# The router's product with the router as the stationary operand: four token groups on four column groups, and one transpose back

## The chip, the cores and the metric

The kernel runs on one core of a Trainium2 chip. Its engines are TensorE (PE in the profile, with its weight loads listed apart as PEld), VectorE (DVE), ScalarE (ACT), GpSimd (POOL), and SyncE (SP), which here only issues DMAs. The metric is the device time of one execution in microseconds (us).

## The reference

The input x has 4 sequences of 1024 tokens with 256 channels. Four blocks follow one another, each on a layer norm of x and each added to x: a retention, a mixture of experts, an RWKV-6 block, and the same mixture of experts again. The change lies in the first two lines of the mixture of experts:

```python
logits = t @ Wg.T + bg                      # t: 4096 x 256, Wg: 8 x 256
probs = jax.nn.softmax(logits, axis=-1)
topw, topi = jax.lax.top_k(probs, K)        # K = 2 of 8 experts
topw = topw / jnp.sum(topw, axis=-1, keepdims=True)
def body(acc, packed):                      # once for each expert
    w1e, w2e, ce = packed
    gate, up = jnp.split(t @ w1e.T, 2, axis=-1)
    return (acc + ce[:, None] * ((silu(gate) * up) @ w2e.T), None)
```

All numbers are float32. The logits are 4096 x 8, once for each of the two mixtures.

## The kernel before

Tokens go in 8 blocks of 512, each of four groups of 128 (NT = 4); channels go in two halves of 128 (KC = 2). The router's logits are made once for each block and each of the two mixtures, so there are 16 calls, and they lie scattered over the stages:

- In the retention stage (up to about 345 us) six calls for the first mixture, put in after chosen chunks of the loop over 32 chunks (lines 1518 and 1531).
- In the first mixture (345 to 570 us) two calls, between expert tiles (line 1558, tiles 7 and 9). This stage goes through 71 tiles of 128 tokens: turn the tile (`fetch`), multiply by w1 (`up`), turn the activation, multiply by w2 (`down`), and scatter.
- In the RWKV stage (about 660 to 1270 us) six calls for the second mixture. That stage is a loop of 64 steps (8 blocks of 8) of scans on VectorE and products on GpSimd, with TensorE's work laid between them by hand (tables `amid`, `late`, `uses`, and lines 1626 to 1629 for the router).
- In the second mixture (from about 1270 us) two calls (lines 1663 and 1558).

One call has four parts. `tokens` normalizes the four groups on ScalarE (line 533). `turned` (line 544) turns them by eight TensorE transposes, and two ScalarE copies bring the result to SBUF as `m_tT`, channels on the partitions (lines 237 and 238). `product` (line 554) multiplies, and `biased` (line 562) adds the bias on VectorE and writes `m_logit`. Outside the RWKV stage `logits` (line 549) runs the first three in a row, and `biased` follows at once. In the RWKV stage they are spread over the steps: `product` is issued at the end of step 8n+19, `biased` in the middle of step 8n+20.

In `product` the turned tokens are the stationary operand (128 x 128) and the router, 128 x 8, is streamed: 8 matmuls, each with its own weight load. A float32 matmul leaves two rows in the trace, so a call has 16 rows of LDWEIGHTS and 16 of MATMUL.

The order on TensorE and ScalarE is the order of the program text everywhere (line 1471). VectorE and GpSimd are ordered by a scheduler in the retention stage and by the text after it (line 1541); SP's queue is ordered by the text in the RWKV stage. [...]

The PSUM tiles named "mm" are a ring of three banks: a new one waits until the one three before it has been read. The router's weight `wr` is loaded by one DMA near the start (line 1457); behind it on SP's queue are the bias and the weights of the retention.

Two other places of the kernel use the form of matmul that the change brings in, a 128 x 32 stationary operand with the result on 32 partitions: the retention's `a_yp` (line 370) and the RWKV stage's `w_varp` (line 1214).

Of the kernel before, what the change touches and what calls it, by code (L numbers as in the profile page):

```python
# [39 lines left out]
F32 = mybir.dt.float32  # L40
# [5 lines left out]
P = 128  # L46
B, T, C = 4, 1024, 256
KC = C // P
BLK = 512
NB = T // BLK  # L50
NT = BLK // P
H, D = 16, 16
GH = P // D
E = 8
# [54 lines left out]
def hybrid_kernel(  # L109
# [24 lines left out]
    nc = tc.nc  # L134
    mm = nc.tensor.matmul
# [3 lines left out]
    def pool(name, side="left"):  # L139
        return tc.alloc_tile_pool(name=name, bufs=1, side=side, reuse_waits="tile")  # L140
# [4 lines left out]
    keep = pool("keep")  # L145
# [3 lines left out]
    def psum(shape, name, tag="mm"):  # L149

        t = ps.tile([P, 512], F32, name=name, tag=tag, bufs=3 if tag == "mm" else 1)
        n = int(np.prod(shape[1:]))
        if len(shape) == 2:
            return t[:, :n]
        return t[:, :n].rearrange("p (a b) -> p a b", b=shape[2])
# [18 lines left out]
    ident = cst[:, O_ID : O_ID + P]  # L174
# [14 lines left out]
    def weight(src, name, where):  # L189
        n = src.shape[1]  # L190
        t = where.tile([P, KC, n], F32, name=name)
        nc.sync.dma_start(out=t, in_=src.rearrange("(k p) n -> p k n", p=P))
        return t
# [296 lines left out]
    class Piece:  # L490
# [58 lines left out]
        def logits(self, n):  # L549
            self.tokens(n)  # L550
            self.turned()
            self.product()

        def product(self):
            tT = self.tT
            lp = self.lp = psum([P, NT, E], "m_lp")
            for i in range(NT):
                for c in range(KC):
                    mm(lp[:, i, :], lhsT=tT[:, c, i * P : (i + 1) * P], rhs=wr[:, c, :],  # L559
                       start=(c == 0), stop=(c == KC - 1))  # L560

        def biased(self, n):
            nc.vector.tensor_add(
                self.logit[:, n * NT : (n + 1) * NT, :], self.lp,
                bias.unsqueeze(1).to_broadcast([P, NT, E]),
            )

# [376 lines left out]
    def rwkv(pi, w):  # L944
# [65 lines left out]
        def deltas(j, parts):  # L1010
# [15 lines left out]
            def mixed(late=False):  # L1026
                for f, c, dp in dps:
# [12 lines left out]
                    if f > 0:  # L1040
                        nc.gpsimd.tensor_add(xf, xf, d["now"][:, c, :])  # L1041

            return [lambda f=f, c=c: product(f, c) for f, c in parts], mixed

        def decay(j):
# [408 lines left out]
            )  # L1454


    wr = weight(router, "wr", keep)
    bias = keep.tile([P, E], F32, name="bias")
    nc.sync.dma_start(out=bias, in_=router_b.partition_broadcast(P))
    ph = pool("ph")  # L1460
# [46 lines left out]
    m, mid = moes[0].pieces[:2]  # L1507
# [42 lines left out]
    def add(j, f, *a):  # L1550
        extra.setdefault(j, []).append((f, *a))

    def pieces_sent(mid, end, logits):

        for i in range(mid.nt):
            add(4 + i, mid.send, i)
        for n, j in logits:
            add(j, end.logits, n)
            add(j, end.biased, n)
        for n in range(PARTS):  # L1560
            add((9, 9, 10, 11, 11, 11)[n], end.route)
        for i in range(end.nt):
            add(12 + i, end.send, i)
        add(6, mid.table, 0)
        add(7, mid.table, 1)
        add(14, mid.table, 2)
        add(18, end.table, 3)
# [44 lines left out]
    extra, mids, fronts = {}, {}, {}  # L1612
# [5 lines left out]
    for n in range(2 * HB - 1):  # L1618
        m = [p for p in moe.pieces if p.start <= n][-1]
        if n == 2 * HB - 2:  # L1620
            add(8 * n + 15, m.block, n - m.start)
            continue
        add(8 * n + 15, m.sums, n - m.start, 0)
        add(8 * n + 16, m.sums, n - m.start, 1)
        fronts[8 * n + 17] = [(m.sums, n - m.start, 2)]
        add(8 * n + 17, m.tokens, n - m.start, True)
        fronts[8 * n + 18] = [(m.turned,)]
        add(8 * n + 19, m.product)
        mids[8 * n + 20] = [(m.biased, n - m.start)]
    mids[44].append((next_a.route,))  # L1630
    add(44, next_a.route)
# [163 lines left out]
```

## Time and profile before

| | us |
|---|---|
| median of 3 runs | 1574.15 |
| lowest and highest of them | 1569.29, 1587.33 |
| the profiled execution, its own time | 1564.52 |
| its span, from the first to the last instruction | 1562.7 |
| busy: PE, DVE, POOL, ACT | 1346.6, 997.7, 892.1, 643.0 |
| mean granted TensorE clock | 0.911 |

Busy time by stage, from the table of windows: in the first 345 us PE is busy for 311.4 and DVE for 205.5; from 345 to 570 us PE for 199.9 and DVE for 101.4; from 660 to 1270 us PE for 501.7, DVE for 540.6 and POOL for 521.6; from 1270 to 1420 us PE for 132.9 and DVE for 61.1. So TensorE leads in the retention and in the mixtures, and VectorE and GpSimd lead in the RWKV stage.

The granted clock is that of TensorE, as a share of full speed. Idle time of an engine that is not the one that holds up the rest costs nothing, so a busy share alone does not tell what an instruction costs.

### The profile page before, as it was taken

Reading aid. Unit: us, or ns where it says so; the run is one execution under the profiler, and the core shown is the slowest. Engines: PE = TensorE matmul, PEld = TensorE weight load, DVE = VectorE, ACT = ScalarE, POOL = GpSimd, SP = SyncE. Lnnn points to the kernel's source line nnn. Section 1 sums busy time; section 2 is a strip of 40 time slices with the busy share of each in tenths; the row PEclk is TensorE's granted clock in tenths of the full one; section 3 lists DMA queues with packets and bytes.
Section 4 is the critical chain, followed back from the end, with each engine's and each line's share of the span. In section 5 each row is a group of like instructions: output and inputs, shape, how many; then the busy total and the mean of one; then the engine's idle time right before and its main releaser. Section 6 shows DMA issues by size and latency. Waiting matters only on the chain.

```text
span 1562.7 us, 21181 instructions
## 1 busy us (share of the span) xinstructions
PE 1346.6 (86%) x6684; PEld 710.2 (45%) x6684; DVE 997.7 (64%) x1914; ACT 643.0 (41%) x1630; POOL 892.1 (57%) x853
## 2 busy tenths in 40 slices
PE   5999999877999989998979798888796677999993
PEld 3667676554656644422233332333332234556561
DVE  6667556535443443299978787979998964433544
ACT  2343434443443333444545454544454224443331
POOL 4233321663573325399988888877799834653231
PEclk9999898978799999998979798979898679899997
DMA  8992111232333431267665454533555932332635
GB/s 291 326 323 84 48 48 42 69 119 69 122 128 100 132 116 54 63 148 190 169 138 148 114 144 109 146 97 108 131 159 135 263 99 67 116 115 85 193 126 185
DMA packets 117549, 207.72 MB, mean 133 GB/s; under 512 B 12192, under 2 KB 80000, under 8 KB 117440
## 3 DMA queue, kind: packets, MB, share of 16 engines
q1 hardware_dynamic: 95904, 160.20, 36.2%
q0 software_dynamic: 17184, 39.86, 8.2%
q10 hardware_dynamic: 4352, 6.29, 1.3%
q8 instruction: 57, 0.93, 0.3%
q14 instruction: 52, 0.43, 0.1%
HBM read 139.18 MB, written 67.14 MB: 132 GB/s over the span
## 4 chain that ended last, share of the span: by engine, by line
PE 56%; DVE 14%; POOL 13%; ACT 7%; issue 5%; DMA 3%; SPq 0%; POOLq 0%; DVEq 0%; ACTq 0%
PE m_hp L836 15%; PE m_op L873 7%; POOL w_s L1168 5%; DVE w_s L1160 5%; PE w_pp L1072 4%; PE a_qkp L311 3%; DVE w_vb L1158 2%; PE a_yp L370 2%; PE w_dp L1020 2%; PE m_xtp L829 2%; PE a_sp L350 2%; PE m_lp L559 2%; PE a_gp L293 2%; POOL xg_all L785 2%; PE m_atp L866 2%
## 5 line engine op out<-in xcount | busy, mean ns | idle before, releaser
L1168 POOL TENSOR_TENSOR w_s<-w_s,w_rT 128x1024 f32<-128x1024 f32 x128 | 304.3, 2412 | 43.2 <-DVE w_s L1160 31.5
L879 POOL DMA_INDIRECT y_all<-m_y,m_to x142 | 137.6, 969 | 284.3 <-ACT m_xt L831 164.9
L836 PE MATMUL m_hp<-w1a,m_xt 128*128 x568 | 285.8, 628 | 11.8 <-ACT m_xt L831 11.0
L842 DVE TENSOR_TENSOR m_a<-m_hp,m_sg 128x256 f32<-128x256 f32 x142 | 60.1, 424 | 266.7 <-ACT m_sg L840 266.7
L1160 DVE TENSOR_TENSOR_SCAN w_s<-w_wk,w_carry,w_vb 128x512 f32<-128x512 f32 x128 | 160.9, 1276 | 18.3 <-ACT w_carry L1178 8.4
L1158 DVE TENSOR_TENSOR w_vb<-w_vb,w_wk 128x1024 f32<-128x1024 f32 x128 | 153.1, 1196 | 17.0 <-ACT w_wk L1101 15.9
L1160 DVE TENSOR_TENSOR_SCAN w_s<-w_wk,w_vb 128x512 f32<-128x512 f32 x128 | 152.9, 1216 | 14.3 <-PE w_yp L1191 7.0
L873 PE MATMUL m_op<-w2a,m_aT 128*128 x568 | 149.2, 386 | 3.9 <-DVE m_aT L868 1.9
L785 POOL DMA_INDIRECT xg_all<-m_row,m_at x128 | 125.4, 980 | 43.7 <-issue 30.4
L836 PEld LDWEIGHTS m_hp<-w1a,m_xt 128*128 128x128 f32 x568 | 103.0, 202 | 87.6 <-issue 74.6
L1191 PE MATMUL w_yp<-w_s,core_c 128*32 128x512 f32 x512 | 93.9, 654 | 41.9 <-POOL w_s L1168 32.7
L840 ACT ACTIVATE m_sg<-m_hp 128x256 f32<-128x256 f32 x142 | 54.5, 384 | 163.6 <-PE m_hp L836 163.6
L323 POOL TENSOR_TENSOR a_t<-a_t,a_t 128x512 f32<-128x512 f32 x32 | 41.1, 1283 | 126.6 <-DVE a_t L322 103.7
L878 ACT ACTIVATE m_y<-m_op,m_share 128x256 f32<-128x256 f32 x142 | 67.3, 474 | 107.1 <-PE m_op L873 106.3
L873 PEld LDWEIGHTS m_op<-w2a,m_aT 128*128 128x128 f32 x568 | 98.2, 193 | 14.1 <-ACT m_y L878 3.0
L1038 POOL TENSOR_TENSOR w_xf<-w_xf,w_sx 128x512 f32<-128x512 f32 x60 | 77.9, 1298 | 35.8 <-ACT w_xf L1037 34.7
L353 DVE TENSOR_TENSOR a_pt<-a_sp,ret_c 128x2048 f32<-128x2048 f32 x32 | 73.2, 2286 | 17.3 <-PE a_sp L350 17.3
L866 PEld LDWEIGHTS m_atp<-cst,m_a 128*128 128x128 f32 x284 | 40.6, 145 | 84.0 <-issue 66.7
L1041 POOL TENSOR_TENSOR w_xf<-w_xf,w_xT 128x512 f32<-128x512 f32 x64 | 69.7, 1090 | 6.1 <-DVE w_xf L1035 1.4
L829 PE MATMUL m_xtp<-cst,m_xg 128*128 128x128 f32 x284 | 57.8, 287 | 13.2 <-DMA m_xg<-xg_all 13.2
L831 ACT COPY m_xt<-m_xtp 128x256 f32<-128x256 f32 x142 | 51.9, 366 | 37.1 <-PE m_xtp L829 37.0
L311 PE MATMUL a_qkp<-wqkv,a_xT 128*128 128x512 f32 x128 | 67.2, 652 | 0.0
(308 smaller groups left out, 2492.6 us busy)
## 6 DMA issues: line engine op xcount, KB each, us to landing
w_vb<-v_all SPq DMA_DIRECT2D x125, 512.0 KB
xg_all<-zero SPq DMA_DIRECT2D x34, 520.0 KB
m_xg<-xg_all SPq DMA_DIRECT2D x34, 520.0 KB
tab<-in_rope SPq DMA_DIRECT2D x32, 512.0 KB
m_back<-y_all SPq DMA_DIRECT2D x48, 256.0 KB
v_all<-w_vT SPq DMA_DIRECT2D x64, 128.0 KB
res<-in_x SPq DMA_DIRECT2D x8, 512.0 KB
w1a<-in_w SPq DMA_DIRECT2D x8, 512.0 KB
```

What stands on the lines that cost most here:

```text
L311: mm(qkp, lhsT=xc[:, c, cols], rhs=wqkv[:, c, 0 : 2 * C], start=(c == 0), stop=(c == KC - 1))
L353: nc.vector.tensor_mul(pts[i].rearrange("p j n t -> p (j n) t"), sp.rearrange("p j n t -> p (j n) t"), causal.unsqueeze(1).to_broadcast([P ...
L785: nc.gpsimd.indirect_dma_start(out=self.moe.sends[2 * (self.start * NT + i) + n][:, :], out_offset=bass.IndirectOffsetOnAxis(ap=self.at[n] ...
L829: nc.tensor.transpose(tp[:, c, :], self.xg[g][:, i, c * P : (c + 1) * P], ident)
L836: mm(hp, lhsT=self.xt[j][:, c, :], rhs=w1a[:, bass.ds(self.ev[j], 1), c, :].rearrange("p o n -> p (o n)"), start=(c == 0), stop=(c == KC - 1))
L873: mm(op, lhsT=self.aT[j][:, c, :], rhs=w2a[:, bass.ds(self.ev[j], 1), c, :].rearrange("p o n -> p (o n)"), start=(c == 0), stop=(c == KC - 1))
L879: nc.gpsimd.indirect_dma_start(out=self.scatters[j][:, :], out_offset=bass.IndirectOffsetOnAxis(ap=self.to[g][:, i : i + 1], axis=0), in_= ...
L1038: nc.gpsimd.tensor_mul(xf, xf, sx)
L1158: nc.vector.tensor_mul(vb, vb, wk[:, 1:2, :].to_broadcast([P, 2, BLK]))
L1160: nc.vector.tensor_tensor_scan(s[:, q, 1 : BLK + 1], wk[:, 0, :], vb[:, q, :], 0.0 if j % NB == 0 else st[j - 1]["carry"][:, n, 2 * h + q ...
L1168: nc.gpsimd.tensor_mul(s[:, :, 0:BLK], s[:, :, 0:BLK], d["r"][:, g, :].unsqueeze(1).to_broadcast([P, 2, BLK]),)
L1191: mm(d["yp", g][32 * q : 32 * q + 32, :], lhsT=w["sel"][:, i, :], rhs=d["s", n, q // 2][:, q % 2, 0:BLK], start=False, stop=(i == 3), skip ...
```

## The change

The router becomes the stationary operand, padded with zeros from 8 to 32 columns. Each of the four groups of 128 tokens streams through one of four column groups of the array, and its logits land, turned, on its own 32 of the 128 partitions of one PSUM tile. A new ScalarE copy brings that tile to SBUF (`m_lT`), and a new TensorE transpose, `flipped`, turns it back so that tokens lie on the partitions again; `biased` reads 8 of each 32 columns. The matmuls are still 8 per call, now with the channel half as the outer loop. A second "mm" tile is taken per call. In the RWKV stage `flipped` is put in the front of step 8n+20, between `product` and `biased`. The load of `wr` now waits for a memset on GpSimd.

```diff
@@ -550,18 +550,27 @@
             self.tokens(n)
             self.turned()
             self.product()
+            self.flipped()
 
         def product(self):
+
             tT = self.tT
-            lp = self.lp = psum([P, NT, E], "m_lp")
-            for i in range(NT):
-                for c in range(KC):
-                    mm(lp[:, i, :], lhsT=tT[:, c, i * P : (i + 1) * P], rhs=wr[:, c, :],
-                       start=(c == 0), stop=(c == KC - 1))
+            lp = psum([P, P], "m_lp")
+            for c in range(KC):
+                for i in range(NT):
+                    mm(lp[32 * i : 32 * i + 32, :], lhsT=wr[:, c, :],
+                       rhs=tT[:, c, i * P : (i + 1) * P], start=(c == 0), stop=(c == KC - 1),
+                       skip_group_check=True)
+            self.lT = ph.tile([P, P], F32, name="m_lT", tag="m_lT", bufs=1)
+            nc.scalar.copy(self.lT, lp)
+
+        def flipped(self):
+            self.lp = psum([P, NT, 32], "m_lpT")
+            nc.tensor.transpose(self.lp.rearrange("p i e -> p (i e)"), self.lT, ident)
 
         def biased(self, n):
             nc.vector.tensor_add(
-                self.logit[:, n * NT : (n + 1) * NT, :], self.lp,
+                self.logit[:, n * NT : (n + 1) * NT, :], self.lp[:, :, 0:E],
                 bias.unsqueeze(1).to_broadcast([P, NT, E]),
             )
 
@@ -1454,7 +1463,9 @@
-    wr = weight(router, "wr", keep)
+    wr = keep.tile([P, KC, 32], F32, name="wr")
+    nc.gpsimd.memset(wr, 0.0)
+    nc.sync.dma_start(out=wr[:, :, 0:E], in_=router.rearrange("(k p) n -> p k n", p=P))
@@ -1626,6 +1637,7 @@
         add(8 * n + 19, m.product)
+        fronts.setdefault(8 * n + 20, []).append((m.flipped,))
         mids[8 * n + 20] = [(m.biased, n - m.start)]
```

## The prediction

> **What bounds the kernel now.** I read the page first, the chain that ended last:
>
> ```profile
> PE 56%; DVE 14%; POOL 13%; ACT 7%; issue 5%; DMA 3%; SPq 0%; POOLq 0%; DVEq 0%; ACTq 0%
> PE m_hp L836 15%; PE m_op L873 7%; POOL w_s L1168 5%; DVE w_s L1160 5%; PE w_pp L1072 4%; PE a_qkp L311 3%; DVE w_vb L1158 2%; PE a_yp L370 2%; PE w_dp L1020 2%; PE m_xtp L829 2%; PE a_sp L350 2%; PE m_lp L559 2%; PE a_gp L293 2%; POOL xg_all L785 2%; PE m_atp L866 2%
> ```
>
> The product to be changed, m_lp at line 559, carries 2% of the chain, some 30 us. That is the ceiling. The view of its tile gives its size:
>
> ```profile
> L559 PEld LDWEIGHTS m_lp<-wr,m_tT x256: 186/192/338, 155.3 to 1331.1; 128*128 128x128 f32 x128
> L559 PE MATMUL m_lp<-wr,m_tT x256: 256/256/383, 155.3 to 1331.2; 128*128 128x8 f32 x128
> ```
>
> These are min/median/max ns. 256 rows over 16 calls are 16 rows per call; each streams only 8 columns, but loads a full 128x128 weight. Now one call after another, in the chain in order of time (start, length), the first call and then the seventh:
>
> ```profile
> 155.35 1.95 PE m_lp L559 x16
> 157.30 1.20 PE a_sp L350 x16
> ```
>
> ```profile
> 398.01 1.98 ACT m_xn L533 x4
> 400.04 0.44 PE m_xtp L237 x2
> 400.48 0.03 issue
> 400.51 3.58 PE m_lp L559 x16
> 404.10 0.52 PE m_xtp L829 x2
> ```
>
> The same 16 rows take 1.95 us in one and 3.58 in the other. The windows around the seventh call tell why (after the busy times, the column before the last two is the granted clock):
>
> ```profile
> 396.90:400.30 3.40, 1.60 (x9) 0.81 (x8) 2.16 (x9) 3.33 (x8) 2.59 (x3) 1.00 1.06 345
> 400.30:403.80 3.50, 3.47 (x18) 3.29 (x17) 0.00 (x0) 0.75 (x2) 2.91 (x6) 0.53 1.05 354
> 403.80:407.20 3.40, 3.40 (x8) 1.85 (x8) 1.83 (x6) 0.37 (x1) 2.05 (x2) 0.50 0.15 55
> 407.20:410.60 3.40, 3.40 (x14) 1.88 (x13) 0.76 (x2) 1.70 (x5) 0.96 (x1) 0.98 0.09 33
> ```
>
> The clock is 1.00 while PE waits for ScalarE and does thin transposes, then half for about 6.8 us, the product included. In one-microsecond windows I find such half-clock stretches at or after all ten calls outside the RWKV stage, in lengths near 3.4, 6.8 and 10.2 us. A call is therefore dear where the clock is halved, and cheap where it isn't.
>
> **What a new product costs.** The nearest row has exactly the new shape: w_varp, eight matmuls of a 128x32 weight with 128 columns, four column groups. The timeline shows one call of it at full clock and one at half:
>
> ```profile
> 828.17 0.66 PE L1214 MATMUL w_varp<-w_sq,tail_c 128*32 128x128 f32 x16
> 1211.11 1.10 PE L1214 MATMUL w_varp<-w_sq,tail_c 128*32 128x128 f32 x16
> ```
>
> A single row lasts 0.27 at full and 0.42 at half clock (273 median, 419 max), so rows follow at (0.66-0.27)/15 = 0.026 us and (1.10-0.42)/15 = 0.045 us. Sixteen rows fall from 1.95 to 0.66, and from 3.58 to 1.10. Were that all, the saving would be 1.3 to 2.5 us a call.
>
> **What takes it back.** First, the loop order. Before, the first two groups used both channel halves, eight rows, before PE needed the second half of m_tT. Now it is needed after four rows. The two copies stand in the timeline around the seventh call:
>
> ```profile
> 399.90 1.21 ACT L238 COPY m_tT<-m_xtp 128x512 f32<-128x512 f32 x2
> ```
>
> The second ends at 401.11, 0.60 after the product started; with the 0.04 that PE needs to follow, the other 12 rows start at 0.64. They end at 0.64 + 11x0.026 + 0.27 = 1.20 (full clock) or 0.64 + 11x0.045 + 0.42 = 1.56 (half). Second, the way back. ScalarE follows PE after 0.09 (the a_tp matmuls end at 159.54, their copy starts at 159.63). A 128x128 copy out of PSUM takes 0.273:
>
> ```profile
> L328 ACT COPY a_vz<-a_vp 128x128 f32<-128x128 f32 x64 | 14.0, 273 | 42.8 <-PE a_vp L315 42.8
> ```
>
> Then 0.04 back to PE, and one transpose, after which the next row can start in 0.11 (0.22 at half clock; m_xtp at 829 is chained at 0.22 for two rows, 0.52 in the slow stretch). PE is free at 1.71 us (full) or 2.18 (half), instead of 1.88 (157.23-155.35) or 3.44 (403.95-400.51). A copy could cost more: the Ln of the same tile takes 0.367, which would take 0.1 a call.
>
> The Trainium skill, "TensorEngine Tiling (Array Packing)", section PSUM Bottleneck, speaks against the change: after a fourfold gain on TensorE the copy out of PSUM may become the bottleneck. The rows agree in kind: of 1.71 us PE works for about 0.75. With TensorE's gain alone I would sum 1.3 x 4 full-clock-like and 2.5 x 6 slow calls, some 20 us; with the wait, less than half. I take the latter. The same page (Key Properties) says that a change of tiling mode drains TensorE. In the trace w_varp starts at 828.17, 0.43 after the start of the 512-column row ahead of it (0.59 long), so entering costs nothing visible; leaving leaves 0.20 without a weight load. By the rule, an estimate from one row's tail (0.27, twice per call) would be 16x0.54 = 9 us, all of the gain; here both switches fall into waits already counted, so I take 0, and keep 0.2 a call (3 us) for the range.
>
> **The sum, call by call** (gain in the time to the next PE work).
> - Retention, calls 1 to 5: 0.2; then 0.5, 0.7, 0.7, where the clock fell in mid-product (2.27, 2.53, 2.62 us before; about 1.7 to 1.8 now, as the work ends before or near the fall); 1.3 for the call at 322 us. Call 6 (345.3 us) is followed by a wait of PE for m_xg until 355.25: 0. Together 3.4.
> - First mixture, at 400 and 415 us: 1.25 each, 2.5.
> - RWKV, at 836, 914, 991, 1067 and 1149 us: off the chain, 0 (below). The sixth, at 1222 us, is on it (3.51 us, then w_rp, for which DVE waited 1.49): its m_tT is there beforehand and ScalarE idles, so 1.10+0.09+0.27+0.04+0.22 = 1.7 in place of 3.4, of which at most 1.5 counts.
> - Second mixture: 0.1 (1278 us, full clock) and 1.0 (1328 us, half for most).
> Sum 8.5 us.
>
> **The RWKV calls, and who stands behind the new waits.** At 836 us:
>
> ```profile
> 836.50 1.95 PE L559 MATMUL m_lp<-wr,m_tT 128*128 128x8 f32 x16
> 838.30 1.10 PE L1238 MATMUL w_rp<-w_rstd,tail_c 128*128 128x512 f32 x2
> 841.37 0.66 DVE L1245 TENSOR_TENSOR w_cen<-w_cen,w_rp 128x512 f32<-128x512 f32 x1
> ```
>
> The new copy stands on ScalarE behind the sums of w_xn and the w_carry copies (until 838.87), so `flipped`, and behind it on PE w_rp and w_twp, start about 1.0 us later. w_rp would end at 840.4 for a reader at 841.37: covered. w_twp ends at 844.0 rather than 843.0, w_tw and w_cen on ScalarE follow 1 us later, and GpSimd's w_sq (845.93 here, 923.53 at the second call, where w_cen ended at 922.63) may be late by some tenths. Bounds 0 and 1.0 a call; I take 0.3 x 5 = 1.5 us lost. If the cover is gone, 5. ScalarE's next work there (w_tw) waits for PE anyway, so the copy's wait holds nothing else up.
>
> **Edits I cost at nothing.** The memset of wr is one of POOL's first (those of the page's start end at 2.5 us), and SP reaches wr's load at 2.74; behind it on SP stand bias, ret_c, wqkv, wgate and the rest, of which wqkv is first needed at 14.84. If the memset came 2 us late, the slack takes it. The DMA moves the same elements. The additional "mm" tile doesn't lengthen any hold: m_lp is freed by the copy, and biased frees m_lpT three allocations before its bank is wanted, as before. 16 copies add 4.4 us to ScalarE, which is idle in those places. biased reads 32 elements as before (0.19 us). In the retention the scheduler could place biased differently on DVE; the next DVE work there, a_pt, waits for later PE work in any case. I leave ±2 us for that.
>
> Net: 8.5 - 1.5 = 7.0 us off. Against the profiled execution's own time, 1564.5 (span 1562.7 and 1.8 around it), that is 1557.5. The median of the runs shown lies 9.6 above that execution; I carry the difference over: 1574.15 - 7 = 1567.
>
> **The rivals.**
> *The half clock goes, too.* The m_lp rows fill about a half to a whole of the slow stretches, with 8 columns a row. If a dense burst ends a stretch one 3.4 us window sooner at six to nine calls, that is 1.7 us each, 10 to 15 more: 1552 to 1557, over 1% faster if the first sum holds as well. For: every stretch begins at transposes and m_lp. Against: the transposes, paced by ScalarE at 0.5 us a pair, stay, and PE now idles during the copy.
> *The half clock spreads.* PE now stands still for 0.4 us in the product and 0.4 in the copy, at each call, and 1 us in the RWKV calls, where the windows from 834 to 843 show 1.00 throughout. The Trainium skill, "TensorE: Matmul & The Clock Gate", section Part 1, has a window of about 3.4 us in which too little activity halves the clock; the trace's stretches agree. Each additional window costs 1.7 us of PE work. Four eat the net gain, and from (15.7+7)/1.7 = 13 windows over 16 calls it is slower by over 1%: 1590. Against it: waits of 4.4 us for w_s (1218 us) are already part of the RWKV stage and it keeps 0.88 on average.
> *It comes back as waits.* If what follows is due to ScalarE or a DMA (as at call 6), the shortened product changes nothing: -2 to +3, 1572 to 1577. Against it: in the mixtures PE is busy 90%, and m_lp stands in the chain with its whole length.
>
> **How the numbers follow.** A change below 1% can't be told from none in runs that spread as these do. Forecast (3 to 14 us off): 0.55. Clock gained: 0.17. Back as waits: 0.14. Clock spread or a chain of late work in the RWKV stage: 0.14. Over 1% faster takes 16 us off: most of the second case and the edge of the first, 0.17. Over 1% slower: most of the last, 0.12. Within: 0.71. The range starts at 1551 (net 7 and nine windows gained, 15.3, and 1 for the copy) and ends at 1583 (four windows lost, 5 in the RWKV stage, 3 for the drains, less 8.5, and the 9 by which a median moves between such runs).
>
> **What would show it.** m_lp at 128*32 with 128 columns, 0.66 to 1.6 us a call from first to last row, with a gap after its fourth row; an m_lT copy of 0.27 on ScalarE; PE free 0.2 us sooner at full and 1.3 at half clock; m_lp's share of the chain below 1%, with ACT m_lT in its place; w_rp 1 us later at the RWKV calls with w_s unmoved. I am wrong if the clock row changes by more than 0.01, or if w_sq starts later in each block of the RWKV stage.

## The result, and the profile after

| | before | after |
|---|---|---|
| median of 17 runs each, us | 1581.08 | 1567.85 |
| lowest and highest | 1569.29, 1590.36 | 1559.89, 1572.42 |
| the profiled execution, its own time and span | 1564.52, 1562.7 | 1572.42, 1570.6 |
| mean granted clock in it | 0.911 | 0.918 |

The ratio of after to before is 0.9922 [0.9903, 0.9942]: some 13 us off, where 7 were forecast. That is within the prediction's 1%, and the interval lies clear of 1. The profiled execution of after was the slowest of its 17, that of before faster than all 17: the two spans can't be subtracted, and below stages are compared instead, with further profiles of both kernels.

The chain that ended last, of the kernel after, by engine and then by line:

```profile
PE 51%; DVE 16%; POOL 15%; ACT 7%; issue 6%; DMA 3%; another core or an unknown queue 1%; SPq 0%; POOLq 0%; DVEq 0%; ACTq 0%
PE m_hp L845 14%; POOL w_s L1177 7%; PE m_op L882 6%; DVE w_s L1169 4%; PE w_pp L1081 4%; PE a_qkp L311 3%; POOL w_xf L1047 2%; PE a_yp L370 2%; DVE w_vb L1167 2%; POOL w_xf L1050 2%; PE m_xtp L838 2%; PE a_gp L293 2%; PE m_atp L875 2%; PE a_op L245 2%; PE a_sp L350 2%
```

The product has left the list of lines. The view of its tile, with the copy that now reads it:

```profile
L561 PEld LDWEIGHTS m_lp<-m_tT,wr x256: 106/110/178, 154.9 to 1330.5; 128*32 128x32 f32 x128
L561 PE MATMUL m_lp<-m_tT,wr x256: 271/273/423, 154.9 to 1330.7; 128*32 128x128 f32 x128
L565 ACT COPY m_lT<-m_lp x16: 247/265/266, 156.2 to 1331.8; 128x128 f32<-128x128 f32 x16
```

So the rows have the shape and the durations of w_varp, and the copy takes 0.265. Now the first call, in the timeline of TensorE (start, length, in brackets the idle time before and what ended it):

```profile
154.90 0.41 PE L561 MATMUL m_lp<-m_tT,wr 128*32 128x128 f32 x4
155.55 0.63 PE L561 MATMUL m_lp<-m_tT,wr 128*32 128x128 f32 x12 [0.23 <-ACT m_tT L238]
156.54 0.33 PE L569 MATMUL m_lpT<-cst,m_lT 128*128 128x128 f32 x1 [0.37 <-ACT m_lT L565]
156.80 0.71 PE L350 MATMUL a_sp<-a_qm,a_kT 32*128 32x256 f32 x8
```

TensorE is free for a_sp 156.80 - 154.90 = 1.90 us after the first row. Before it was 1.88. At full clock the new product saves nothing at all: the two waits, 0.23 and 0.37, and the transpose eat the whole gain of the rows. So at a call like this one nothing of the 13 us comes from a shorter product.

What changed shows behind the call. First the kernel before, in 1 us windows around it (PE, PEld, DVE, ACT and POOL busy, then the granted clock, the DMA share and GB/s):

```profile
154.00:155.00 1.00, 0.89 (x5) 0.42 (x6) 1.00 (x6) 1.00 (x3) 0.92 (x3) 1.00 0.00 0
155.00:156.00 1.00, 0.97 (x8) 0.73 (x8) 1.00 (x7) 0.88 (x2) 0.84 (x3) 1.00 0.00 0
156.00:157.00 1.00, 1.00 (x11) 1.00 (x10) 0.56 (x4) 0.00 (x0) 1.00 (x2) 1.00 0.09 16
157.00:158.00 1.00, 1.00 (x18) 0.93 (x18) 0.19 (x1) 0.00 (x0) 0.76 (x5) 1.00 0.00 0
158.00:159.00 1.00, 1.00 (x11) 0.57 (x4) 0.46 (x1) 0.00 (x0) 0.96 (x1) 0.57 0.00 0
159.00:160.00 1.00, 1.00 (x4) 0.67 (x3) 1.00 (x1) 0.37 (x2) 0.20 (x1) 0.50 0.00 0
160.00:161.00 1.00, 1.00 (x2) 0.34 (x1) 0.83 (x1) 1.00 (x4) 0.00 (x0) 0.50 0.00 0
161.00:162.00 1.00, 1.00 (x3) 0.53 (x2) 0.00 (x0) 0.01 (x1) 0.00 (x0) 0.73 0.00 0
```

And the kernel after:

```profile
155.00:156.00 1.00, 0.77 (x16) 0.41 (x16) 1.00 (x7) 0.49 (x1) 0.84 (x4) 1.00 0.06 16
156.00:157.00 1.00, 0.63 (x9) 0.34 (x9) 0.20 (x2) 0.27 (x1) 0.85 (x2) 1.00 0.00 0
157.00:158.00 1.00, 1.00 (x17) 0.65 (x15) 0.10 (x1) 0.00 (x0) 0.91 (x3) 1.00 0.00 0
158.00:159.00 1.00, 1.00 (x6) 0.76 (x7) 0.98 (x1) 0.37 (x2) 0.71 (x2) 1.00 0.00 0
159.00:160.00 1.00, 1.00 (x3) 0.38 (x2) 1.00 (x1) 1.00 (x3) 0.00 (x0) 1.00 0.00 0
160.00:161.00 1.00, 1.00 (x5) 0.57 (x3) 1.00 (x3) 0.00 (x1) 0.00 (x0) 1.00 0.00 0
```

From 157 us on TensorE is busy throughout in both, but before, the clock is halved from 158.1 to 161.5, over the dense matmuls that follow the call; after, it isn't, although TensorE stood idle for more of the call itself (0.77 and 0.63 busy). A stretch of 3.4 us at half clock is 1.7 us of work. The starts of a_sp mark the steps of the retention, so their distances price each step. In us, for the step in which a call stands and the step behind it (`before_again` and `whole_again` are second profiles of before and after; `rwkv_only`, which keeps the old product in these calls, and the two fillers are told of below):

| | before | before_again | rwkv_only | after | whole_again | thin_fill | dense_fill |
|---|---|---|---|---|---|---|---|
| call 1, behind it | 14.0, 7.3 | 14.0, 7.4 | 14.0, 5.7 | 14.0, 5.7 | 14.0, 5.7 | 15.9, 8.4 | 15.4, 5.7 |
| call 2, behind it | 11.4, 12.3 | 11.1, 10.9 | 12.1, 11.6 | 11.1, 9.3 | 11.1, 9.3 | 12.4, 9.3 | 12.4, 9.3 |
| call 3, behind it | 15.4, 12.8 | 14.8, 11.9 | 14.8, 10.2 | 14.8, 10.2 | 14.8, 10.2 | 16.2, 11.8 | 16.2, 10.2 |
| call 4, behind it | 11.2, 10.7 | 11.1, 10.9 | 12.0, 9.9 | 10.7, 9.7 | 10.7, 10.4 | 14.2, 10.5 | 11.9, 9.7 |
| call 5, behind it | 18.4, 10.5 | 19.0, 10.0 | 17.9, 9.7 | 18.1, 10.2 | 17.7, 9.0 | 20.6, 9.3 | 19.5, 7.6 |
| from the a_sp near 132 us to the last | 204.4 | 205.4 | 199.4 | 198.1 | 193.0 | 208.9 | 198.9 |
| lost clock in it | 18.8 | 17.1 | 13.7 | 8.5 | 8.5 | 17.1 | 5.1 |

"Lost clock" is the sum of 1 minus the granted clock over all 1 us windows, that is, the work at full clock that was not done. From before_again to after, the calls' own steps give 0 + 0 + 0 + 0.4 + 0.9 = 1.3 us, the steps behind them 1.7 + 1.6 + 1.7 + 1.2 - 0.2 = 6.0: three of them are just half of 3.4. Together that is the 7.3 us from 205.4 to 198.1, while the lost clock falls by 8.6. (In before_again, after, whole_third and staged two steps without a call, near 290 and 300 us, last about 2 us longer each than in the other profiles, 10.5 to 10.9 against 8.5 and 8.9; why is open. These kernels ran where the kernel before has a median of 1581; the other runs are compared with medians of 1557 or 1558. So 193.0 and 198.1 are the same kernel, and only kernels of one chip are subtracted; whole_third, on the chip of before_again, has the steps of after to within 0.1.)

The half clock does not follow every old product. Behind calls 1 and 3 of rwkv_only the clock stays full, and only calls 2 and 4 lose it. Take calls 1 to 4 of each profile. In the three with the old product, ten of these twelve calls have a half-clock stretch that begins within 3.4 us of the product's start. In four with the new one (after and whole_again, and whole_third and outside_only, which come below) one call of sixteen has it, the fourth of outside_only.

Part of this is position. In one trace the stretches begin whole multiples of 3.41 us apart: in before at 158.13, 175.20, 229.81 and 253.70, which is 5, 16 and 7 times 3.41. Count these marks back from a stretch. Before's first product (155.35 to 157.23) then lies between two marks, 154.72 and 158.13, and the clock falls at the second. That of rwkv_only (156.00 to 157.88) lies across the mark at 156.39, and no fall follows. The new product of after (154.90 to 156.80) lies between the marks 154.48 and 157.90, as before's does, and the clock stays full. This is one comparison, worked out from the clock in three traces, and no run was made for it.

The gain is not an accident of the profiles, either. Each timed execution has its mean granted clock on record. The medians are 0.916 before and 0.926 after the change on the chip of whole_again, 0.913 and 0.923 on that of whole_third, 0.915 and 0.922 on that of outside_only. As shares of the time these differences are 16, 16 and 11 us, where the medians of the times differ by 18.6, 14.4 and 14.1.

### The profile page after: what moved, and what is told of

Its sections match the earlier page's. It is cut to its first block, busy times and chain, and to the rows that moved or that the text cites. A ratio compares the mean times of both kernels' runs of the same rounds, so it can differ in the third digit from the quotient of the medians.

```text
span 1570.6 us, 21231 instructions
## 1 busy us (share of the span) xinstructions
PE 1323.9 (84%) x6700; PEld 680.1 (43%) x6700; DVE 997.4 (64%) x1914; ACT 645.7 (41%) x1646; POOL 892.1 (57%) x854
## 4 chain that ended last, share of the span: by engine, by line
PE 51%; DVE 16%; POOL 15%; ACT 7%; issue 6%; DMA 3%; another core or an unknown queue 1%; SPq 0%; POOLq 0%; DVEq 0%; ACTq 0%
PE m_hp L845 14%; POOL w_s L1177 7%; PE m_op L882 6%; DVE w_s L1169 4%; PE w_pp L1081 4%; PE a_qkp L311 3%; POOL w_xf L1047 2%; PE a_yp L370 2%; DVE w_vb L1167 2%; POOL w_xf L1050 2%; PE m_xtp L838 2%; PE a_gp L293 2%; PE m_atp L875 2%; PE a_op L245 2%; PE a_sp L350 2%
## 5 line engine op out<-in xcount | busy, mean ns | idle before, releaser
L1177 POOL TENSOR_TENSOR w_s<-w_s,w_rT 128x1024 f32<-128x1024 f32 x128 | 304.5, 2415 | 39.3 <-DVE w_s L1169 29.5
L1167 DVE TENSOR_TENSOR w_vb<-w_vb,w_wk 128x1024 f32<-128x1024 f32 x128 | 153.1, 1196 | 17.1 <-ACT w_wk L1110 15.9
L353 DVE TENSOR_TENSOR a_pt<-a_sp,ret_c 128x2048 f32<-128x2048 f32 x32 | 73.2, 2286 | 17.1 <-PE a_sp L350 17.0
L875 PE MATMUL m_atp<-cst,m_a 128*128 128x128 f32 x284 | 55.7, 278 | 9.0 <-DVE m_a L851 5.7
```

The source lines that it names most:

```text
L875: nc.tensor.transpose(tp[:, c, :], self.act[j][:, c * P : (c + 1) * P], ident)
L1167: nc.vector.tensor_mul(vb, vb, wk[:, 1:2, :].to_broadcast([P, 2, BLK]))
L1177: nc.gpsimd.tensor_mul(s[:, :, 0:BLK], s[:, :, 0:BLK], d["r"][:, g, :].unsqueeze(1).to_broadcast([P, 2, BLK]),)
```

## The experiments

**The RWKV calls alone, and all the others alone.** In `rwkv_only` the ten calls outside the RWKV stage keep the old product, in `outside_only` the six inside it do:

```diff
-            self.product()          # in logits(), for rwkv_only
-            self.flipped()
+            self.product_old()
...
-        add(8 * n + 19, m.product)  # for outside_only
-        fronts.setdefault(8 * n + 20, []).append((m.flipped,))
+        add(8 * n + 19, m.product_old)
```

> The change in the RWKV stage's six calls alone; the ten other calls keep the old product. If the gain is PE time and clock outside the RWKV stage: 0.998 to 1.002 of before, w_s unmoved, PE waiting about 2 us for m_lT at five calls. If the RWKV stage gives a share of the 13 us: 0.994 to 0.997, and its stretch is shorter by 5 us or more.

> The change in the ten calls outside the RWKV stage alone. If the gain lies there: 0.990 to 0.995 of before, like the whole change. If the RWKV stage gives a share: 0.996 or more. The retention's first four calls should show the granted clock at 1.00 behind them, as in the profile of the whole change.

Measured: 1557.96, 1.0009 [0.9991, 1.0027], and 1543.39, 0.9897 [0.9857, 0.9937]. All of the gain is outside the RWKV stage. It was expected that the clock stays full behind calls 1 to 4 of outside_only; behind three of them it does, and the fourth lost 3.4 us. In the RWKV stage TensorE's next work does wait, as the timeline of the kernel after shows at its first call of that stage:

```profile
842.60 0.62 PE L561 MATMUL m_lp<-m_tT,wr 128*32 128x128 f32 x16
844.98 0.26 ACT L565 COPY m_lT<-m_lp 128x128 f32<-128x128 f32 x1
845.29 0.33 PE L569 MATMUL m_lpT<-cst,m_lT 128*128 128x128 f32 x1 [2.08 <-ACT m_lT L565]
845.46 1.02 PE L1247 MATMUL w_rp<-w_rstd,tail_c 128*128 128x512 f32 x2
```

The copy stands behind ScalarE's older work until 844.98, so w_rp comes 2.86 after the product's start instead of 1.81, and the time doesn't notice. Between the two kernels, on one chip, the retention differs by 199.4 - 193.3 = 6.1 us (lost clock 13.7 and 8.5). From there to the bias of the first RWKV call the difference is 507.8 - 500.0 = 7.8 (lost clock 39.3 and 29.0): here the stretches behind the mixture's two calls became fewer as well. For the other pair, before_again and `whole_third`, that second part was 515.1 and 515.3 with the same lost clock, 34.1 in both: it comes and goes with the clock.

**One column group.** `one_group` makes the router the weight as well, but with two groups of tokens per matmul, 256 columns, and all on one column group; the copy is then 32 x 512, and four transposes go back:

```diff
+            for h in range(2):
+                cols = slice(2 * h * P, (2 * h + 2) * P)
                 for c in range(KC):
+                    mm(lp[0:32, cols], lhsT=wr[:, c, :], rhs=tT[:, c, cols],
+                       start=(c == 0), stop=(c == KC - 1))
...
+            for i in range(NT):
+                nc.tensor.transpose(
+                    self.lp[:, i, :], self.lT[:, i * P : (i + 1) * P], ident[0:32, 0:32])
```

> The router as the weight, but all tokens on one column group: four matmuls of 128x32 by 256 columns, about 1.9 us of dense streaming (before: 1.95 us of thin rows), then a copy of 0.59 and four transposes. Theory of PE time: PE is free at about 3.0 us instead of 1.9, so 1.003 to 1.008 of before, and half-clock stretches stand at the retention's first four calls as before. Theory of the clock: dense streaming keeps the clock at 1.00 at these four calls, which spares about 12 us there and leaves 0.996 to 1.000.

Measured: 1553.87, 0.999 [0.9971, 1.001]. The clock stays full at the first four calls here, too (the steps behind calls 1 and 3 last 5.8 and 10.2), but the steps with these calls are 14.9, 11.9, 15.7 and 11.5: 0.8 to 0.9 above the whole change. The retention is 4.1 us longer than that of outside_only on the same chip (197.4 and 193.3), as the longer calls say. The rest of the difference lies behind it and was not followed up. Of the two forms tried, only the one with four groups at once gains time.

**The way back twice.** Copy and transpose are done a second time, with the same output:

```diff
             nc.tensor.transpose(self.lp.rearrange("p i e -> p (i e)"), self.lT, ident)
+            nc.scalar.copy(self.lT, self.once)
+            nc.tensor.transpose(self.lp.rearrange("p i e -> p (i e)"), self.lT, ident)
```

> The whole change with the copy and the transpose done twice in a row. If the way back costs what the sum says (0.09 + 0.27 + 0.04 + 0.11 = 0.5 us of standing PE at each of the ten calls outside the RWKV stage, hidden in the others): 4 to 6 us over the whole change, 0.995 to 0.997 of before. If standing still brings the half clock back at the retention's first four calls: 0.999 to 1.003.

Measured: 1558.71, 1.0005 [0.9983, 1.0028]; the whole gain is gone, which is the second of the two outcomes named. The calls' steps grew by 0.7 (14.7, 11.8, 15.5), which is the second way back itself; the steps behind calls 1 and 3 went back to 7.3 and 11.8, the values with half clock, and call 4 lost 3.4 us of clock; call 2 stayed at full clock. A little more standing and one more transpose after the dense rows were enough to bring it back at three calls of four.

**Thin rows or dense rows in the same place.** This pair asks for the clock alone. Both kernels are the whole change with a filler between product and way back, at the ten calls outside the RWKV stage; its result is not used. `thin_fill` repeats the old product's 16 rows of 8 columns, `dense_fill` takes 8 rows of 256 columns:

```diff
+            for i in range(NT):                      # thin_fill
+                for c in range(KC):
+                    mm(pad[:, 8 * i : 8 * i + 8], lhsT=tT[:, c, i * P : (i + 1) * P],
+                       rhs=wr[:, c, 0:E], start=(c == 0), stop=(c == KC - 1))
...
+            for i in range(2):                       # dense_fill
+                for c in range(KC):
+                    mm(pad, lhsT=tT[:, c, i * P : (i + 1) * P], rhs=tT[:, c, 0 : 2 * P],
+                       start=(c == 0), stop=(c == KC - 1))
```

> The whole change once more, beside three variants of it on one chip. From the ten calls alone (0.9897) and the six alone (1.0009): 0.989 to 0.993 of before. Its first profile was slower than its median, with waits of 5 to 12 us on ScalarE that no other profile has; if these are chance, they are gone here and the retention's last call lies 6 us or more ahead of before. If they belong to the change, they come back.

> At the ten calls outside the RWKV stage, the old product's 16 thin rows (about 1.95 us) are added between the new product and the transpose, into unused PSUM columns; the copy of m_lT lies beneath them. Theory of PE time: 1.95 less the 0.4 of the copy that they cover, 15 us over the whole change in sum, 1.000 of before, the same as dense_fill. Theory of the clock: the half-clock stretches come back at the retention's first four calls, and it is slower than dense_fill by 5 us or more.

> The same with 8 dense rows (4 matmuls of 128x128 by 256 columns, about 1.75 us) in place of the thin ones. Theory of PE time: as thin_fill, within 2 us. Theory of the clock: 1.00 at the retention's first four calls, fewer half-clock stretches in the first mixture too, and a time at least 5 us below thin_fill, 0.990 to 0.996 of before.

Measured: whole_again 1539.39, 0.9897 [0.9855, 0.9938]; thin_fill 1564.84, 1.0046 [1.0028, 1.0064]; dense_fill 1552.69, 0.998 [0.9962, 0.9999]. The fillers differ by 12 us, though at full clock they keep TensorE equally long (1.95 us for the thin rows at call 2, 1.99 for the dense ones at call 1). dense_fill stayed above the 0.990 to 0.996 that was expected of it. The windows of thin_fill behind its first call:

```profile
159.00:160.00 1.00, 1.00 (x16) 0.57 (x8) 0.00 (x0) 0.00 (x0) 0.00 (x0) 0.50 0.00 0
160.00:161.00 1.00, 1.00 (x8) 0.71 (x5) 0.57 (x1) 0.00 (x0) 0.00 (x0) 0.50 0.00 0
161.00:162.00 1.00, 1.00 (x3) 0.54 (x3) 1.00 (x1) 0.50 (x2) 0.00 (x0) 0.50 0.00 0
162.00:163.00 1.00, 1.00 (x3) 0.43 (x2) 0.72 (x1) 0.87 (x3) 0.00 (x0) 0.50 0.00 0
```

And those of dense_fill:

```profile
160.00:161.00 1.00, 1.00 (x18) 0.72 (x16) 0.19 (x1) 0.00 (x0) 0.64 (x2) 1.00 0.00 0
161.00:162.00 1.00, 1.00 (x9) 0.69 (x6) 0.74 (x1) 0.12 (x1) 0.00 (x0) 1.00 0.00 0
162.00:163.00 1.00, 1.00 (x4) 0.47 (x3) 1.00 (x1) 1.00 (x4) 0.00 (x0) 1.00 0.00 0
```

TensorE counts as busy in both; the clock column differs. In the retention dense_fill is 10.0 us shorter (198.9 and 208.9) at 12.0 less lost clock, and over the 22 timed executions of each the median clock is 0.931 against 0.918. So what stands in the call bears on the clock: 16 thin rows in this place bring the half clock back at calls 1, 3 and 4 (not at call 2), 8 dense ones at none of the four.

**The copy's wait covered.** `flip_later` puts other work of TensorE between product and way back, so that nothing stands still for the copy. The second block's logits of the first mixture also move one tile ahead:

```diff
             self.product()
-            self.flipped()
+            later.append(self)
...
             scores(i)
+            flips()
```

> The transpose back is put behind the next work of PE (the scores of the next chunk, the up product of the next tile), so PE never stands still for the copy; in the RWKV stage the product moves up to the front of step 8n+19. If standing still costs only its own length: 0.4 us at nine calls, 3 to 5 us below the whole change. If it also calls the half clock (way_back_twice lost 13 us where 5 were expected): 5 to 12 us below. If the RWKV stage's waits of 2 us on PE cost nothing, its stretch stays as in the whole change.

Measured: 1542.11, 0.9898 [0.9866, 0.9929], the same as whole_again beside it, so neither of the two gains named came. Its retention is 2.5 us shorter (190.5 and 193.0), but before the bias of the first RWKV call that is lost again, with 34.1 us of lost clock there against 29.8. Hiding the 0.4 us for the copy did not pay by itself.

**The stages of a call spread over a step.** `staged` goes further: outside the RWKV stage, transposes, product and way back each come behind another stretch of TensorE's work, so that each copy has one to run beside. In the mixtures the second block's logits are asked for a tile sooner, and in the first of them the routing starts a tile later:

```diff
             self.tokens(n)
-            self.turned()
-            self.product()
-            self.flipped()
+            stages.append(("turned", self, n))
...
             scores(i)
+            hook("flipped")
...
             rest(i)
+            hook("turned")
...
             results(i)
+            hook("product")
```

> The kernel before, unchanged, for one look beside the others on this chip. If half clock at the retention's first four calls is the kernel's and not chance, its 1 us windows show 0.50 at or after each of the calls near 157, 176, 231 and 255 us, as the first profile did, and a lost clock (sum of 1 minus the granted clock) near 19 us from 150 to 345 us, against 11.6 to 14.5 in the two profiles of the change. If those stretches fall by chance, it shows a lost clock of 14 or less there.

> The change as it is, on the chip of the next kernel: 0.990 to 0.992 of the kernel before, by the two comparisons there are.

> The stages of a call outside the RWKV stage are spread over one step of the loop each: transposes of the tokens after one stretch of matmuls, product after the next, way back and biased after the next, so that TensorE stands still for no copy of ScalarE's. If the half-clock stretches that are left come from the transposes paced by ScalarE, they vanish at calls 5 to 8 and the time falls 8 to 20 us below the whole change (0.978 to 0.985 of the kernel before). If they come from other things around the calls, or later logits delay the routing, it stays within 4 us of the whole change (0.988 to 0.995).

Measured: before 1581.03, before_again 1573.81, whole_third 1566.64, 0.9899 [0.9863, 0.9936]; staged 1555.02, 0.9826 [0.9786, 0.9867]. It has the lowest ratio of all, and is 11.6 below whole_third on the same chip. before_again, a single execution, repeats the half clock at all of calls 1 to 4 (17.1 lost from 150 to 345 us); with rwkv_only's two calls of four, the half clock is frequent with the old product and not certain. The number that was expected for staged came, but not by the reason given: from 150 to 440 us the lost clock is 14.8 + 12.5 = 27.3 in staged and 11.4 + 15.9 = 27.3 in whole_third. The half-clock stretches that are left did not vanish there. What went at the calls is the waiting. The timeline of whole_third at the first call's transposes:

```profile
153.51 1.91 PE L237 MATMUL m_xtp<-cst,m_xn 128*128 128x128 f32 x8
155.46 0.41 PE L561 MATMUL m_lp<-m_tT,wr 128*32 128x128 f32 x4
156.10 0.63 PE L561 MATMUL m_lp<-m_tT,wr 128*32 128x128 f32 x12 [0.23 <-ACT m_tT L238]
```

And staged at the third:

```profile
229.38 1.04 PE L237 MATMUL m_xtp<-cst,m_xn 128*128 128x128 f32 x8
232.83 0.64 PE L579 MATMUL m_lp<-m_tT,wr 128*32 128x128 f32 x16
234.48 0.33 PE L587 MATMUL m_lpT<-cst,m_lT 128*128 128x128 f32 x1
```

The transposes no longer go at ScalarE's pace (1.04 in place of 1.91), and product and way back take 0.64 + 0.33 in place of 1.90. That is 2.01 against 3.8, 1.8 us a call; five such calls make 9 us, and the retention fell by 198.1 - 190.9 = 7.2, of which 1.7 is lost clock (8.5 and 6.8). Over whole executions the clock has a larger part: its median is 0.926 in staged and 0.923 in whole_third, some 5 us. How the 11.6 divide between waiting and clock was not separated further.

**The old product in the staged order.** This asks whether the new product is worth anything there:

> The staged order with the old product (16 rows of 8 columns, no way back; the router's tile stays padded). Staged with the new product stood at 0.983 of the kernel before. If staging saves the standing of TensorE whatever the product is, and the product itself is worth no more than some tenths of a microsecond a call, this stands at 0.981 to 0.988. If the thin rows bring half clock back in the staged order as well, as they did in the filler, the retention keeps a lost clock of 12 us or more (6.8 with the new product) and the whole stands at 0.989 to 0.997.

Measured: 1549.31, 0.9945 [0.9917, 0.9973]. Its retention, from the a_sp near 132 us to the last, loses 13.7 us of clock, against 6.8 in staged (on another chip): the second theory. The median clock of its executions, 0.915, is that of before beside it, 0.916, so the order alone saves waiting and no clock. The order alone is worth 0.5%, the product alone 1%, both together 1.7%.

## Why the prediction was right or wrong

The time came in within the range, by luck: the shorter product, which was to bring 8.5 us, brought 1 to 3, and the clock, which was taken as given, brought most of the rest.

- *PE free at 1.71 us (full clock) instead of 1.88.* Measured 1.90. The twelve rows ended at 1.28 instead of 1.20, the copy's wait was 0.36 instead of 0.40, and the transpose handed TensorE on after 0.26 where I took 0.11, the spacing of rows of the same kind. Rows, copy and order of events were as forecast.
- *At half clock 2.18 instead of 3.44.* Measured 3.13 and 3.19 at the seventh and eighth calls of after, 2.40 at the eighth of whole_again. In after the transpose there follows only 2.86 after the first row; some 0.8 of it lies between the rows' end in the record and the copy's start, which the trace doesn't explain.
- *Retention 0.2, 0.5, 0.7, 0.7, 1.3.* From before to after, first row to next work: 0, 0.3, 0.6, 0.6, 0.9; from before_again 0, 0, 0, 0.4, 0.9. *First mixture 1.25 each*: 0.3 and 0.2. *Sixth RWKV call 1.5*: 3.39 us against 3.44; in after two rows of w_yp, which stood ahead of the product before, lie between its rows. *Second mixture 0.1 and 1.0*: 0 and -0.1. Against the first profile of before these gains add up to about 3 us, against the second to about 1, where 8.5 stood.
- *RWKV: 1.0 later, mostly covered, with 1.5 given back on the sixth call's gain.* It was 1.05 later at four calls and sooner at the fifth (1.17 us), and the stage's part of the time is 1.0009. The net of nothing came, but by two errors that cancel: the sixth call gained 0.05, not 1.5, and the delays cost nothing that the time shows, not 1.5.
- *Memset and DMA at nothing*: nothing to be seen against it. *Drains at nothing*: the place read for it shows no change of form, as the row ahead of w_varp at 828.17 is w_mp of line 1006, itself a 128*32 form. Where the form does change, at a_yp behind a_op (150.90 us in before), the first row starts 0.31 after the one ahead, where rows of a_op follow one another at 0.22. Behind the way back, a_sp (a 32*128 form) starts 0.26 after the transpose, where w_rp (128*128, at 845.46) starts 0.17 after it. That is about 0.1 us for a change, an estimate from these two places, inside the 0.2 a call that the range held.
- *Some 30 us as the ceiling*: the product's own share of the chain is no ceiling for what it costs. Of the 7.3 us that the retention gained, 6.0 lie in the steps behind the calls.
- *The half clock goes, too* (10 to 15 more, chance 0.17) is nearest to what happened, without most of the first sum: at most of calls 1 to 4 the stretch did not end sooner, it did not begin at all. It was argued down with the copy's wait and the transposes' pace, both of which are indeed there; I had set the chance by what the change adds to the idle time, where the thin rows that it removes weighed more. This is the step that failed: the clock was taken as given and the product re-priced under it, while the product was part of what sets the clock. *The half clock spreads* was a real risk all the same: the second way back spends the whole gain.
- The sign that I named for it, a change of the clock row by more than 0.01, was too coarse. The row moved by 0.007 in both pairs (0.911 to 0.918, 0.916 to 0.923), and 0.007 of 1566 us is 11 us.

The Trainium skill's section PSUM Bottleneck ("TensorEngine Tiling (Array Packing)") proved stricter than I took it: way back and waits used up all of the rows' gain at full clock. Its "TensorE: Matmul & The Clock Gate", Part 1, puts the halving down to how busy TensorE has been, over windows of some 3.4 us; the stretches here have 3.4, 6.8 or 10.2, but the profile's busy share is not that busyness: it was 0.89 to 1.00 in the five windows ahead of the fall at 158 us.

Left open: which of the call's rows count for the clock, and how many, and how much the position of a call among the 3.41 us marks decides. Thin rows against dense ones were told apart, transposes and standing still only together.

## What to carry to other kernels

Where the granted clock halves, look at what TensorE did in the few microseconds before, and price small work by the step behind it, not by its own length: thin matmuls in a chain paced by another engine can halve the clock behind them, 1.7 us of work for each stretch of 3.4. Short rows alone don't make a call shorter while each hands over to a copy. Dense rows gave 1% here, spreading the stages over other work of TensorE 0.5%, both together 1.7%. The mean clock moves little for it: by 0.010 here, which is worth 16 us.

## What was not expected of the hardware

- 16 rows of 8 columns or 8 rows of 256 in the same place, both shown as a busy TensorE for as long: 12 us of the time, with 12 us less lost clock in the retention.
- At full clock the 16 new rows take 0.62, and their product with its waits 1.90; at 397 us in after, at half clock, the copy began 0.8 after the rows' recorded end, and not so at 401 us in whole_again.
- One kernel on two chips: 1539.39 and 1566.64 for the whole change, 1558 and 1581 for the kernel before; the ratios agree (0.9897, 0.9899).
